# A four-layer state-space network: softplus in another PSUM buffer, side work in turns, and a last epilogue in four streams

## The chip, the cores and the metric

The kernel runs on one core of a Trainium2 chip: TensorE (PE), VectorE (DVE), ScalarE (ACT), GpSimd (POOL), and SyncE (SP), which issues the DMAs. The metric is the time of one execution in device microseconds (us); lower is better. The kernel is written with tiles and pools. A scheduler at build time puts the instructions of each engine in an order, chooses the buffer of each tile and adds the waits; the engines then work through their fixed queues.

## The reference

Eight images of 48 x 48 positions and 96 channels pass through four layers, each `x = x + ss2d(group_norm(x))`. Cut to what matters, a layer computes:

```python
xz = x @ in_proj_w.T                       # 96 -> 2 * 192
xc, z = split(xz)
xc = silu(depthwise_conv3x3(xc) + conv_b)
xs = four sequences of xc: row order, column order, both reversed
dts, B, C = split(xs @ x_proj)             # rank 6 or 16, then 16, 16
delta = softplus(dts @ dt_proj + bias)
h = exp(delta * A) * h + delta * u * B     # along 2304 positions, 16 states
y = sum over states of h * C, + D * u
y = layer_norm(sum of the four directions) * silu(z)
x = x + y @ out_proj_w.T
```

The last layer writes the same scan as `decay * cumsum(dB_u / (decay + 1e-12))` with `decay = exp(cumsum(delta * A))`. With these inputs, decay is so small after the first positions that the kernel computes the sums at the ends of each sequence alone; a flag checks this on the chip, and only where it fails the whole last layer is run again.

## The kernel before

Images go in pairs: 4 layers with 4 pairs each, named `(l, p)`. The 192 inner channels of two images are three tiles of 128 partitions: 128 channels of each image, and the last 64 channels of both.

A pair has three parts. The **prologue** (line 276) loads x, computes the group norm, the input projection, the 3 x 3 convolution (nine matmuls for each of five row chunks and each of three tiles, line 301), silu, and the x projections, whose results go to DRAM. The **units** are the scans, for each tile, phase and direction (12 groups). In layers 0 to 2 a unit is one state of a chunk of 768 positions. In the last layer (`Edge`, line 825) a group has four units, each with four states of 192 positions (`EDGE`): `decay` makes four exponentials da (880), `spread` makes rq with Ln and Exp (887, 888) and spreads B over the partitions with four matmuls into a PSUM tile b (893), `scan` multiplies twice on DVE (898, 899), runs four scans (901) and multiplies twice on POOL (905, 906), and `add_up` sums into acc with identity matmuls (913), four units later (`LAG`). `prepare` (563) computes softplus for a group: a matmul (585), six ACT operations (590 to 601), two on POOL (603, 604), one on DVE (607), a copy to dl (609) and the product du (611, 614); in the last layer a scan over dl follows (839). The **epilogue** (942) takes the pair's y from DRAM in 16 chunks of 144 positions: a first sum over channels subtracts the mean (956 to 962), copy and square (996, 997), a second sum over channels, Ln and Exp (1006, 1007), product (1009), scale (1012), gate projection (1018, 1022), silu (259, with a table load ahead of it and one behind, 260), product (1031), output projection with transposition (1057 to 1059), copy (1063), and two DMAs to the output.

`run` (1114) writes all this in one program order. In unit k it readies unit k+1, scans unit k and adds up unit k-4. Then it takes side steps: each `yield` in a prologue or epilogue ends one step. `behind` is the epilogue of the pair before, `ahead` the prologue of the next. `side_step` takes a step of that side which holds a PSUM bank (its last step yielded True), or of the one that has made the smaller share of its total; a prologue step can also be refused (`GATED`) until the units have come to tile t. In layers 0 to 2 there is at most one side step for each unit, in the last layer ten. What remains is drained at the last group of a pair. After all units, the last pair's epilogue is drained by itself (line 1211).

PSUM[...]: pool `pacc` one buffer of two banks (acc), `pb` two buffers of two banks (b), `psum` two buffers of one bank (`bank()`), which serve softplus, prologue and epilogue. In SBUF the epilogue has two buffers each for ex and ey (`sm2`) and one each for exn and eyc (`sm1`); `tmp` has three large buffers, which the prologues use.

`keep_order(a, b)` (1100) adds an order between all neighbours on each engine, over the instructions number a to b as written. `mark()` notes the current number. It is called before the first unit, and at unit 0 of every pair in the last layer; `keep_order(*marks[:2])` so holds layers 0 to 2 to the written order. What lies outside, the scheduler may reorder.

Of the kernel before, what the change touches and what calls it, by code (L numbers as in the profile page):

```python
# [102 lines left out]
def ss2d_layers_kernel(ctx: ExitStack, tc: tile.TileContext, x_in, consts, weights, out):  # L103
# [158 lines left out]
    def bank():  # L262
        return psum.tile([P, BANK], F32, name="ps", tag="ps")
# [299 lines left out]
    def prepare(c):  # L563
        l, p, t, ph, d = c.l, c.p, c.t, c.ph, c.d
        ly, s = layers[l], state[l, p]
        k, r = ph + 2 * d, ly.rank
        c.dl = ddpool.tile([P, SCAN], F32, name="dl", tag="dl")[:, : c.m]
        c.du = ddpool.tile([P, SCAN], F32, name="du", tag="du")[:, : c.m]
        u = s["u"][t]
        if ph == 1:  # L570
            u = u.rearrange("p (h w) -> p w h", w=W)
        if c.dts is None:
            load_dt(c)
        dts = c.dts
        for z in range(0, c.m, HALF):
            m = min(HALF, c.m - z)
            at = slice(z, z + m)

            ps = bank()
            v = ps[:, :m]  # L580
            for b in c.batches:
                q0 = 32 * b if t == 2 else 0
                o = ps[64 * b : 64 * b + 64] if t == 2 else ps
                chans = slice(P, DIN) if t == 2 else slice(0, P)
                nc.tensor.matmul(  # L585
                    o[:, :m], ly.dtw[q0 : q0 + r, k, chans], dts[q0 : q0 + r, at],
                    start=True, stop=True,
                )
            yield
            nc.scalar.activation(v, v, AF.Identity, bias=ly.column(t, C_DTB + k))  # L590


            e = sm1.tile([P, HALF], F32, name="e", tag="e")[:, :m]
            nc.scalar.activation(e, v, AF.Abs)
            nc.scalar.activation(e, e, AF.Exp, scale=-1.0)
            yield
            lg = sm1.tile([P, HALF], F32, name="lg", tag="lg")[:, :m]
            nc.scalar.activation(lg, e, AF.Ln, bias=ones)
            w1 = sm1.tile([P, HALF], F32, name="w1", tag="w1")[:, :m]
            nc.scalar.activation(w1, e, AF.Identity, bias=ones)  # L600
            nc.scalar.activation(w1, w1, AF.Identity, bias=minus)  # L601
            yield
            nc.gpsimd.tensor_sub(lg, lg, w1)  # L603
            nc.gpsimd.tensor_add(lg, lg, e)  # L604
            yield
            yield
            nc.vector.scalar_tensor_tensor(v, v, 0.0, lg, ALU.max, ALU.add)
            yield
            nc.scalar.copy(c.dl[:, at], v)
            if ph == 0:  # L610
                nc.vector.tensor_mul(c.du[:, at], v, u[:, c.c0 + z : c.c0 + z + m])  # L611
            else:
                r0 = (c.c0 + z) // H
                nc.vector.tensor_mul(
                    c.du[:, at].rearrange("p (w h) -> p w h", h=H),
                    v.rearrange("p (w h) -> p w h", h=H),
                    u[:, r0 : r0 + m // H, :],
                )
            if z + m == c.m and l == NLAYER - 1:
                c.sum_up()  # L620
            if z + m == c.m:
                yield
# [29 lines left out]
    class Chunk:  # L652
# [47 lines left out]
        def load(self, n):  # L700

            s, m, at = state[self.l, self.p], self.m, slice(self.c0, self.c0 + self.m)
            if n == 0:
                self.brow = rpool.tile([2 * NR, SCAN], BF16, name="brow", tag="brow")
                for j, b in enumerate(self.batches):
                    nc.sync.dma_start(
                        self.brow[NR * j : NR * j + NR, :m],
                        s["xb"][self.ph, b, :, self.d, :, at],
                    )
            row = 2 * layers[self.l].rank + 2 * NS * self.d + NS + n  # L710
            self.cb[n] = cb = cbpool.tile([P, SCAN], F32, name="cb", tag="cb")
            for b in self.batches:
                o = cb[64 * b : 64 * b + 64] if self.t == 2 else cb
                rows = s["xd"][self.ph, b, row : row + 1, at]
                nc.sync.dma_start(
                    o[:, :m], rows.to_broadcast([64 if self.t == 2 else P, m])
                )
# [221 lines left out]
                nc.sync.dma_start(s["yd"][t], y)  # L939


    def epilogue(l, p):
        ly, s = layers[l], state[l, p]
        gn, yd, src = s["gn"], s["yd"], x_store(l, p)
        dst = x_store(l + 1, p) if l + 1 < NLAYER else None
# [5 lines left out]
        def over_channels(ps, z, own, own_2, tiles):  # L951


            for t in tiles:
# [4 lines left out]
                for b in range(2):  # L959
                    o = ps[half(b), 2, :]  # L960
                    nc.tensor.matmul(o, off[:, 0:64], z[:, b, :], start=True, stop=False)  # L961
                    nc.tensor.matmul(o, own_2[:, half(b)], z[:, 2, :], start=False, stop=True)

        def three():
            return bank()[:, : 3 * EM].rearrange("p (t m) -> p t m", t=3)

        loaded = {}

        def load(i):
            at = slice(ECHUNKS[i][0], sum(ECHUNKS[i]))  # L970
            x = sm2.tile([DM, 2, EM], F32, name="ex", tag="ex")
            nc.sync.dma_start(x, src[:, :, at].rearrange("b c m -> c b m"))
            y = sm2.tile([P, 3, EM], F32, name="ey", tag="ey")
            nc.sync.dma_start(y, yd[:, :, at].rearrange("t p m -> p t m"))
            loaded[i] = x, y

        load(0)
        for _ in range(3):
            yield
        for i, (c0, m) in enumerate(ECHUNKS):  # L980
            at = slice(c0, c0 + m)
            x, y = loaded.pop(i)

            ps = three()
            over_channels(ps, y, centre, centre_22, (0, 1))
            yield True
            over_channels(ps, y, centre, centre_22, (2,))
            xn = sm1.tile([DM, 2, EM], F32, name="exn", tag="exn")
            for b in range(2):
                nc.scalar.activation(  # L990
                    xn[:, b, :], x[:, b, :], AF.Identity,
                    bias=gn[:, b, 1:2], scale=gn[:, b, 0:1],
                )
            yield True
            yc = sm1.tile([P, 3, EM], F32, name="eyc", tag="eyc")
            nc.scalar.copy(yc, ps)
            nc.scalar.activation(y, ps, AF.Square)
            yield
# [22 lines left out]
            for b in range(2):  # L1021
# [1 line left out]
                    ps[half(b), 2, :], ly.inw[:, DIN + P : 2 * DIN], xn[:, b, :],  # L1023
                    start=True, stop=True,
                )
            if i + 1 < len(ECHUNKS):
                load(i + 1)
            yield True
            silu(ps, ps)
            yield True  # L1030
# [18 lines left out]
                continue  # L1049

            q = m // 2
            ps = bank()[:q, : 4 * DM].rearrange("q (h b c) -> q h b c", h=2, b=2)
            for h in range(2):
                z = slice(h * q, h * q + q)
                for b in range(2):
# [10 lines left out]
                    out[2 * p + b, at, :].rearrange("(h q) c -> q h c", h=2), st[:, :, b, :]  # L1066
                )
            yield
        del state[l, p]


    def drain(g):
        for _ in g:
            pass
# [22 lines left out]
    def mark():  # L1097
        marks.append(len(tc._region_blocks()[0].instructions))

    def keep_order(a, b):  # L1100

        last = {}
        info = mybir.DependencyInfo(mybir.DependencyClass.NoSync, mybir.DependencyReason.DATA)
        for i in tc._region_blocks()[0].instructions[a:b]:
            if i.engine in ENGINES:
                if i.engine in last:
                    tc.add_manual_dep(i, last[i.engine], info, reason="order")
                last[i.engine] = i.name
# [5 lines left out]
    def run(pairs, short):  # L1114
# [53 lines left out]
        for k, ((l, p, unit), c, n) in enumerate(todo):  # L1168
            at = pairs.index((l, p))
            following = pairs[at + 1] if at + 1 < len(pairs) else None  # L1170
            if l in short and unit == 0:
                mark()
            per = NS // QUAD if l in short else NS
            all_units = len(groups) * (per if l in short else len(SCANS) * per)
            place["tiles"] = 3 * unit // all_units
            if done:
                behind, done = Side(epilogue(*done), 195), None
            if unit == LAG and following:
                ahead = Side(begin(*following), 300)
            if n == 0:  # L1180
                drain(coming)
                if unit + per == all_units:
                    drain(behind.g)
                    drain(ahead.g)
                coming_to = chunks.index(c) + 1
                coming = prepare(chunks[coming_to]) if coming_to < len(chunks) else iter(())
            if n == max(0, per - 1 - DECAYS):
                drain(coming)
            if n == 10 and coming_to + 1 < len(chunks):
                z = chunks[coming_to + 1]  # L1190
                if (z.l, z.p) == (l, p):
                    load_dt(z)
            busy = collected()
            get_ready(k + 1)
            catch_up()
            c.scan(n)
            if k >= LAG:
                (bl, bp, _), b, bn = todo[k - LAG]
                b.add_up(bn)
                if todo[k - LAG + 1][0][:2] != (bl, bp):  # L1200
                    done = bl, bp
            step(coming)

            for _ in range(10 if l in short else 0 if busy else 1):
                side_step(rest) or side_step(behind, ahead)
        for _, c, n in todo[-LAG:]:
            collected()
            c.add_up(n)
            catch_up()
        collected()  # L1210
        drain(epilogue(*pairs[-1]))

    last = NLAYER - 1
    run([(l, p) for l in range(NLAYER) for p in range(NPAIR)], (last,))

    keep_order(*marks[:2])


    every = sm1.tile([P, 1], F32, name="every", tag="every")
# [102 lines left out]
```

## Time and profile before

| what | us |
|---|---|
| time, median of 3 runs | 21290.81 (21287.53 to 21323.55) |
| time of the profiled execution | 21306.41 |
| its span | 21304.6 |
| mean granted clock of TensorE in it | 0.944 |

The profile comes from one execution, taken by the hardware profiler. Its page gives the busy time of each engine over the span, and the span in 40 equal slices, about 533 us each, in which a digit is the busy share in tenths. The trace behind it can be asked for stretches (start and end, length, then for each engine busy time and number of instructions in it, then the granted clock of TensorE as a share of full speed, the mean busy share of the DMA engines, and GB/s), for the waits (which engine at which line waited for which, in total, how often, and the longest), for the chain of waits that ended last (start, duration, engine and line), and for single instructions. An fp32 matmul has two records in the trace. The dearest groups of the last layer's lines, from 18400 us to the end (busy us, mean ns; the rest of the row is idle time before them):

| line | what | records | busy us | mean ns |
|---|---|---|---|---|
| 301 | PE, convolution, 128 x 480 | 990 | 412.4 | 557 |
| 901 | DVE, scan, 128 x 192 | 768 | 363.7 | 532 |
| 913 | PE, acc | 1536 | 355.5 | 378 |
| 905, 906 | POOL, products, 128 x 768, each | 192 | 347.4 | 1816, 1810 |
| 880 | ACT, da, 128 x 192 | 768 | 293.0 | 442 |
| 887, 888 | ACT, rq, 128 x 768 | 192, 192 | 176.1, 158.7 | 925, 833 |
| 898, 899 | DVE, products with b | 192, 192 | 181.4, 182.3 | 955, 955 |
| 259, 260 | ACT, table loads | 101, 101 | 129.6, 129.6 | 1283, 1283 |

Records overlap each other, so a mean times a count can exceed the busy time.

### The profile page before, as it was taken

The numbers are of one execution on the slowest core, as the hardware profiler recorded it, in microseconds if no ns is written. First come the engines' busy times: TensorE is split into PE (matmuls) and PEld (weight loads), VectorE is DVE, ScalarE is ACT, GpSimd is POOL, SyncE is SP. The second block draws the span as 40 slices with busy tenths as digits, with TensorE's granted clock in tenths as the row PEclk, the third lists the DMA queues.
The fourth block names the chain that finished last, engine by engine and source line by source line (L and its number), as shares of the span: only waits on it lengthen the run. The fifth ranks groups of instructions, "written<-read, shape, count | busy, mean of one in ns | idle before, by whom it ended". The sixth has DMA issues, their size and how long they took to land. (4 is left out here: it accounts for less than half of the span.)

```text
span 21304.6 us, 229326 instructions
## 1 busy us (share of the span) xinstructions
PE 18651.1 (88%) x64610; PEld 9183.5 (43%) x64610; DVE 18839.5 (88%) x15938; ACT 13518.2 (63%) x23969; POOL 17988.3 (84%) x11081
## 2 busy tenths in 40 slices
PE   8988988998998998998998988988988988988886
PEld 3333443443443443443443443443443443444555
DVE  6999999999999999999999999999999999997453
ACT  5655666666666665665665666665665665666776
POOL 5989898888899899899898889889889888896442
PEclk8999999999999999999999999999999999999887
DMA  4666676676676676676676666666666666664221
GB/s 136 195 190 192 190 196 192 188 192 193 190 198 195 187 200 193 187 202 196 187 200 192 191 193 195 186 194 194 186 195 192 187 194 191 189 193 124 78 72 52
DMA packets 1707633, 3832.97 MB, mean 180 GB/s; under 512 B 238448, under 2 KB 575216, under 8 KB 1693168
## 3 DMA queue, kind: packets, MB, share of 16 engines
q1 hardware_dynamic: 1706352, 3818.21, 61.5%
q8 instruction: 521, 8.54, 0.2%
q14 instruction: 760, 6.23, 0.1%
HBM read 3665.08 MB, written 152.27 MB: 179 GB/s over the span
## 5 line engine op out<-in xcount | busy, mean ns | idle before, releaser
L804 PE MATMUL acc<-cb,cst 128*128 128x384 f32 x27648 | 10772.4, 519 | 0.0
L768 POOL TENSOR_TENSOR cb<-cb,da 128x768 f32<-128x768 f32 x5184 | 9350.0, 1813 | 1586.3 <-DVE da L759 953.8
L804 PEld LDWEIGHTS acc<-cb,cst 128*128 128x128 f32 x27648 | 5031.9, 197 | 3972.4 <-issue 1530.2
L759 DVE TENSOR_TENSOR_SCAN da<-da,carry,b 128x768 f32<-128x768 f32 x3456 | 6267.3, 1813 | 219.0 <-DVE b L755 1.4
L755 DVE TENSOR_TENSOR b<-du,b 128x768 f32<-128x768 f32 x5184 | 4910.0, 947 | 789.6 <-PE b L743 780.1
L726 ACT ACTIVATE da<-dl,a 128x768 f32<-128x768 f32 x5184 | 4770.6, 926 | 94.0 <-POOL cb L768 61.2
L743 PE MATMUL b<-brow,pick 48*128 48x512 bf16 (+3 forms) x10368 | 2660.3, 338 | 1516.2 <-DVE da L759 1184.7
L726 ACT ACTIVATE b<-dl,a 128x768 f32<-128x768 f32 x1728 | 1560.5, 903 | 2927.1 <-DVE da L759 2673.6
L768 POOL TENSOR_TENSOR cb<-cb,bb 128x768 f32<-128x768 f32 x1728 | 3133.2, 1813 | 188.1 <-issue 63.6
L698 POOL TENSOR_TENSOR bb<-bb,du 128x768 f32<-128x768 f32 x1728 | 3131.4, 1812 | 124.5 <-DMA bb<-xd 78.8
L759 DVE TENSOR_TENSOR_SCAN da<-da,b 128x768 f32<-128x768 f32 x1728 | 3029.5, 1753 | 107.4 <-DVE b L755 0.9
L743 PEld LDWEIGHTS <-pick 48*128 48x128 bf16 (+1 forms) x10368 | 667.2, 97 | 4345.3 <-DVE da L759 2285.7
L759 DVE TENSOR_TENSOR_SCAN bb<-b,carry,bb 128x768 f32<-128x768 f32 x1152 | 2069.7, 1797 | 9.1 <-ACT b L726 6.1
L301 PE MATMUL ps<-pad,diag 128*128 128x480 f32 (+1 forms) x4320 | 1995.8, 560 | 17.0 <-DVE du L611 11.5
L650 ACT COPY carry<-da 128x1 f32<-128x1 f32 x3456 | 626.9, 181 | 1068.6 <-DVE da L759 1055.7
L590 ACT ACTIVATE ps<-ps,w 128x384 f32<-128x384 f32 (+1 forms) x912 | 496.6, 545 | 1115.0 <-PE ps L585 1114.4
L301 PEld LDWEIGHTS ps<-pad,diag 128*128 128x128 f32 x4320 | 807.4, 192 | 721.1 <-issue 293.4
L603 POOL TENSOR_TENSOR lg<-lg,w 128x384 f32<-128x384 f32 (+1 forms) x912 | 891.5, 977 | 196.7 <-ACT w L601 196.6
L759 DVE TENSOR_TENSOR_SCAN bb<-b,bb 128x768 f32<-128x768 f32 x576 | 999.2, 1735 | 15.5 <-ACT b L726 11.9
L585 PE MATMUL ps<-dts,w 6*128 6x384 f32 (+5 forms) x2432 | 819.7, 522 | 182.0 <-DVE du L611 65.9
L604 POOL TENSOR_TENSOR lg<-lg,e 128x384 f32<-128x384 f32 (+1 forms) x912 | 889.3, 975 | 71.2
L798 PE MATMUL acc<-y,cst 128*128 128x384 f32 x1008 | 625.3, 751 | 275.2 <-ACT y L819 176.2
(141 smaller groups left out, 17322.1 us busy)
## 6 DMA issues: line engine op xcount, KB each, us to landing
cb<-xd SPq DMA_DIRECT2D x4736, 384.0 KB
cb<-xd SPq DMA_DIRECT2D x4736, 192.0 KB
bb<-xd SPq DMA_DIRECT2D x1152, 384.0 KB
bb<-xd SPq DMA_DIRECT2D x1152, 192.0 KB
yd<-y SPq DMA_DIRECT2D x48, 1152.0 KB
ey<-yd SPq DMA_DIRECT2D x256, 216.0 KB
brow<-xb SPq DMA_DIRECT2D x576, 72.0 KB
ex<-xs SPq DMA_DIRECT2D x256, 108.0 KB
```

The costliest lines, as they stand in the source:

```text
L301: nc.tensor.matmul(ps[:, :m], ly.diag[:, int(t == 2), j, :], pad[:, r0 + dy : r0 + dy + nr, dx : dx + W], start=(j == 0), stop=(j == 8),)
L585: nc.tensor.matmul(o[:, :m], ly.dtw[q0 : q0 + r, k, chans], dts[q0 : q0 + r, at], start=True, stop=True,)
L603: nc.gpsimd.tensor_sub(lg, lg, w1)
L604: nc.gpsimd.tensor_add(lg, lg, e)
L650: nc.scalar.copy(*late_act.pop(0))
L698: nc.gpsimd.tensor_mul(b, b, self.du)
L726: nc.scalar.activation(da, self.dl, AF.Exp, scale=columns_of(self.l, self.t, self.ph, self.d, n))
L743: nc.tensor.matmul(b[:, z : z + zm], w, self.brow[:k, z : z + zm], start=True, stop=True)
L755: nc.vector.tensor_mul(b, self.du, b)
L759: nc.vector.tensor_tensor_scan(way(h), way(da), way(b), start, ALU.mult, ALU.add)
L768: nc.gpsimd.tensor_mul(c, c, h)
L804: nc.tensor.matmul(self.acc[:, a, : self.m // 2], ident, c[:, a, :], start=False, stop=(n == NS - 1 and not self.turns),)
```

## The change

All of it concerns the last layer. In `prepare`, softplus of a group of 192 positions takes its PSUM tile from `pb` (tag b) in place of `psum`. In each unit of the last layer, `ahead` gets eight tries and `behind` five, one after the other in turns, in place of ten steps by share. `epilogue` gets `part` and `parts`: a stream takes every fourth chunk. Streams 0 and 1 take their PSUM banks from `psum`, 2 and 3 from `pb`; stream 0 keeps its small buffers and its load ahead, while streams 1 to 3 have x, xn, y and yc in one buffer of `tmp` and load at the start of a chunk. The last epilogue runs as four such streams, one step of each in turn. `mark()` is called ahead of them and after them, and a second `keep_order` takes the marks with index 2 and 3. Epilogues of other pairs have `part=0, parts=1`.

```diff
@@ -576,7 +576,8 @@
-            ps = bank()
+
+            ps = pb.tile([P, 2 * BANK], F32, name="b", tag="b") if c.m == EDGE else bank()
             v = ps[:, :m]
@@ -939,7 +940,8 @@
-    def epilogue(l, p):
+    def epilogue(l, p, part=0, parts=1):
+
...
+        def own_bank():
+            return bank() if part < 2 else pb.tile([P, 2 * BANK], F32, name="b", tag="b")
+
         def three():
-            return bank()[:, : 3 * EM].rearrange("p (t m) -> p t m", t=3)
+            return own_bank()[:, : 3 * EM].rearrange("p (t m) -> p t m", t=3)
 
         loaded = {}
 
         def load(i):
             at = slice(ECHUNKS[i][0], sum(ECHUNKS[i]))
-            x = sm2.tile([DM, 2, EM], F32, name="ex", tag="ex")
+            if part:
+                w = tmp.tile([P, 10 * EM], F32, name="ew", tag="tmp")
+                x, xn = (
+                    w[:DM, a * EM : a * EM + 2 * EM].rearrange("p (b m) -> p b m", b=2)
+                    for a in (0, 2)
+                )
+                y, yc = (
+                    w[:, a * EM : a * EM + 3 * EM].rearrange("p (t m) -> p t m", t=3)
+                    for a in (4, 7)
+                )
+            else:
+                x = sm2.tile([DM, 2, EM], F32, name="ex", tag="ex")
+                y = sm2.tile([P, 3, EM], F32, name="ey", tag="ey")
+                xn = yc = None
             nc.sync.dma_start(x, src[:, :, at].rearrange("b c m -> c b m"))
-            y = sm2.tile([P, 3, EM], F32, name="ey", tag="ey")
             nc.sync.dma_start(y, yd[:, :, at].rearrange("t p m -> p t m"))
-            loaded[i] = x, y
-
-        load(0)
+            loaded[i] = x, y, xn, yc
+
+        mine_of = range(part, len(ECHUNKS), parts)
+        load(part)
         for _ in range(3):
             yield
-        for i, (c0, m) in enumerate(ECHUNKS):
+        for i in mine_of:
+            c0, m = ECHUNKS[i]
             at = slice(c0, c0 + m)
-            x, y = loaded.pop(i)
+            if i not in loaded:
+                load(i)
+            x, y, xn, yc = loaded.pop(i)
...
-            if i + 1 < len(ECHUNKS):
-                load(i + 1)
+            if not part and i + parts < len(ECHUNKS):
+                load(i + parts)
...
-            ps = bank()[:q, : 4 * DM].rearrange("q (h b c) -> q h b c", h=2, b=2)
+            ps = own_bank()[:q, : 4 * DM].rearrange("q (h b c) -> q h b c", h=2, b=2)
...
-            for _ in range(10 if l in short else 0 if busy else 1):
+            if l in short:
+                for i in range(8):
+                    side_step(ahead)
+                    if i < 5:
+                        side_step(behind)
+            elif not busy:
                 side_step(rest) or side_step(behind, ahead)
...
         collected()
-        drain(epilogue(*pairs[-1]))
+        mark()
+        streams = [epilogue(*pairs[-1], part, 4) for part in range(4)]
+        while streams:
+            streams = [g for g in streams if next(g, g) is not g]
+        mark()
 
     last = NLAYER - 1
     run([(l, p) for l in range(NLAYER) for p in range(NPAIR)], (last,))
 
     keep_order(*marks[:2])
+    keep_order(*marks[2:4])
```

Left out are the lines that make exn and eyc only where the stream has none, and the release of a pair's state once all its streams have ended.

More of the change, by code (lines that the diff above doesn't have):

```diff
@@ L987, in epilogue @@
             over_channels(ps, y, centre, centre_22, (2,))
-            xn = sm1.tile([DM, 2, EM], F32, name="exn", tag="exn")
+            if xn is None:
+                xn = sm1.tile([DM, 2, EM], F32, name="exn", tag="exn")
             for b in range(2):
@@ L994, in epilogue @@
             yield True
-            yc = sm1.tile([P, 3, EM], F32, name="eyc", tag="eyc")
+            if yc is None:
+                yc = sm1.tile([P, 3, EM], F32, name="eyc", tag="eyc")
             nc.scalar.copy(yc, ps)
@@ L1068, in epilogue @@
             yield
-        del state[l, p]
+        state[l, p]["left"] = state[l, p].get("left", parts) - 1
+        if not state[l, p]["left"]:
+            del state[l, p]
     def drain(g):
```

## The prediction

> **What bounds the kernel now.** I read the page's busy shares and 40 slices first, to find where the touched code runs.
>
> ```profile
> PE 18651.1 (88%) x64610; PEld 9183.5 (43%) x64610; DVE 18839.5 (88%) x15938; ACT 13518.2 (63%) x23969; POOL 17988.3 (84%) x11081
> ...
> PE   8988988998998998998998988988988988988886
> DVE  6999999999999999999999999999999999997453
> ACT  5655666666666665665665666665665665666776
> ```
>
> For 36 slices VectorE is at nine tenths and ScalarE near six. The last three or four slices are another regime: DVE falls to 7, 4, 5 and 3, ACT rises to 7. That is the last layer, the only place that the edit touches, about 1,915 of 21,305 us. So I cut it by pair (the 192 scans of line 901 in each give the borders) and took the busy times of each stretch: pairs 0, 1, 2, 3, then the last epilogue.
>
> ```profile
> 19390.00:19790.00 400.00, 348.08 (x1762) 235.79 (x1763) 219.23 (x384) 319.10 (x588) 185.53 (x125) 0.91 0.31 86
> 19790.00:20240.00 450.00, 372.36 (x2016) 257.68 (x2016) 225.55 (x394) 351.95 (x652) 191.43 (x134) 0.89 0.27 75
> 20240.00:20690.00 450.00, 375.44 (x1992) 259.12 (x1991) 227.59 (x398) 350.24 (x660) 192.50 (x135) 0.87 0.26 73
> 20690.00:21063.00 373.00, 252.08 (x1603) 207.87 (x1603) 213.06 (x375) 291.29 (x556) 183.95 (x119) 0.80 0.24 67
> 21063.00:21305.00 242.00, 158.88 (x1042) 135.40 (x1041) 20.36 (x35) 118.24 (x190) 1.80 (x1) 0.73 0.13 34
> ```
>
> Columns: length, PE, weight loads, DVE, ACT, POOL, clock, DMA. In pairs 0 to 2 PE (83%) and ACT (78%) are both near full and wait for each other; in pair 3 ACT leads; in the tail nobody does, and the clock is 0.73. The chain of waits of the tail shows why:
>
> ```profile
> 21140.12 1.28 ACT L259
> 21141.85 1.02 ACT eyc L1012 x2
> 21153.83 1.28 ACT L259
> 21155.55 1.02 ACT eyc L1012 x2
> 21167.51 1.28 ACT L259
> ```
>
> The table load for silu comes every 13.7 us, once a chunk: a chain PE, ACT, PE, ACT, DVE, ACT, PE with one chunk in flight. The waits, first of the tail, then of the pairs (us in total, times, longest):
>
> ```profile
> DVE eyc L1009 <- ACT ps L1007: 172.1, 16, 16.2
> ```
> ```profile
> PE b L893 <- DVE rq L901: 80.3, 37, 7.8
> ...
> PE ps L585 <- DVE du L611: 18.5, 4, 4.8
> ```
> ```profile
> ACT dl L609 <- DVE ps L607: 53.0, 27, 5.8
> ```
>
> The second says that PE, in order, already waits for a free buffer of b; the third is PE waiting for a bank that softplus holds; the last is ScalarE standing in softplus for GpSimd and VectorE.
>
> **What the skill says.** The Trainium skill, "TensorE: Matmul & The Clock Gate", What's actually happening: the array runs at half rate until about 3.4 us of sustained work. The trace agrees: the 24 output records of a tail chunk (L1057 to L1059), after an idle PE, come every 0.16 us, inside busy stretches (at 19930.4 us) every 0.083 us. "ScalarE: Activation LUTs", What ACT_TABLE_LOAD costs: 1,283 ns and a drain of about 1,380. The trace has 1,283 ns and no drain beside it: the silu starts 0.01 us after its load. "Perfetto Trace Analysis", Tensor Engine Instruction (MATMUL, LD_WEIGHTS): ScalarE, VectorE and GpSimd are strict FIFO. So the place of an instruction in its queue decides what a wait blocks, which the waits above bear out.
>
> **Tail.** One chunk costs, from the timeline at 21150 to 21164 us: first over_channels A 2.0 us of PE, second B 1.9, gate C 1.16, output 3.8 cold or 1.9 warm. ScalarE: two exn 0.91, copy and square 1.06, Ln and Exp 1.11, scale 1.01, load, silu, load 3.08, eo 0.47; sum 7.64. Sixteen chunks at 13.67 are 219 us. The four streams advance in turns, and the changed program's instruction order on PE and ScalarE is phase by phase: four A's, four B's, four C's, four silus, four outputs. From the end of the fourth silu: DVE and the last output 2.7 us; four A's 7.9; four B's 7.6; last Ln, Exp 2.2; four scales 4.05; four silus 12.3 less the closing load 1.28, 11.0. That is 35.5 us for four chunks. copy, square, C and exn lie beside PE's or ScalarE's longer phase. Streams 1 to 3 have no prefetch: their loads (324 KB, where 216 KB took 2.65 us on the chain) begin when their buffer is free, and are covered by the next A of stream 0. I add 2.5 us a round for what of this and of the cold clock shows: 38 us, four rounds 152, and 5 at the start for four loads in place of one. Gain 219-157 = 62. Bounds: 35.5 gives 77; 43 (outputs cold at 1.9 more, loads exposed by 4, and 1.6 for refilled queues) gives about 46. All 32 table loads remain.
>
> **Which instructions keep their order.** run() marks the first unit once, then the first unit of every pair of the last layer, then both ends of the streams: numbers 0, 1 to 4, 5 and 6. keep_order(*marks[2:4]) hence spans pair 1 of the last layer, from its first unit to pair 2's, and not the streams; these the scheduler orders, in phases as told. In pair 1 every queue, SP's too, now follows the written order.
>
> **Pairs 0 and 2.** Before, ten side steps a unit were shared by progress: 40 units x 10 = 400, while a prologue has 259 and an epilogue 195 (counted yields). The remaining 54, among them most of the 44 steps of the x projections, were poured out at unit 44. Slices of 50 us show it (line 901's scans, then all engines):
>
> ```profile
> 20200.00:20250.00 50.00, 3.77 (x8) 0.77 0.31 91
> ```
> ```profile
> 20200.00:20250.00 50.00, 30.94 (x198) 24.15 (x199) 12.78 (x25) 33.05 (x58) 6.47 (x10) 0.77 0.31 91
> ```
>
> There are 8 scans where 192 in 450 us make 21, and PE has 31 of 50 us. After, 8 x 40 and 5 x 40 finish both by unit 44. Filling that hole is worth 20 to 25 us a pair (PE 31 instead of 44 of 50 us, and its follow-up). Against it stands softplus in b: it holds one of two buffers from L585 to L611, 6.8 us in the trace (19912.4 to 19919.2), once in four units, so the next b waits. DVE, 3.8 us a unit in units of 8.7, hides most; I take 1 us a group, 11 groups, +10. Net -12 each. Bounds: -45 (all hidden, the freed bank lets convolution and epilogue overlap), +25 (4 us a group, half the hole).
>
> **Pair 1.** The same hole, -20. In written order softplus stands in one piece: after the silu (3.08) and a convolution's eviction (0.65) come six ScalarE operations 2.4, two GpSimd 1.2, DVE 0.37, ACT 0.30, DVE 0.36: 8.4 us. PE has four convolution matmuls (3.3) before a wait for the bank and three after it, then the b that needs softplus's buffer. It stands about 4 to 6 us; behind it are acc, convolution and the epilogue's matmuls, and ScalarE waits for those. 11 groups x 4.5 = 50. Net +30. Below: nothing more than the hole, if queues run ahead (-30); above: 6 us a group, and 25 us each for the chains of the group norm and of the projections, whose DMAs landed in up to 4.7 us on the chain of waits (+95).
>
> **Pair 3.** No prologue: before, ten steps a unit finished the epilogue by unit 27 at 9.7 us a unit (14.6 us a chunk, the tail's chain again), and 24 units ran at 5.4. After, five steps a unit last to unit 43. ACT's 291 us less 9 bare units at 3.5 is 260 over 39 units, 6.65; at 88% busy 7.56. 39 x 7.56 + 9 x 5.4 = 344 against 373: -30. Bounds -60 (full ScalarE) and 0 (the chain still paces).
>
> Sum: -12+30-12-30-62 = -86. Against the profiled execution, 21306.4 (span 21304.6 and 1.8 around it), 21220; that run was 15.6 over the median of 21290.8, so I forecast 21205.
>
> **Rivals.** (1) The two free banks let PE run warm and full in all pairs: PE's 372 us at 96% is 388 instead of 450, of which I would believe half: pairs 0 to 2 -35, -10, -35, pair 3 -45, tail -70: -195, 21096. For it: clock 0.88 while PE is 83% busy. Against: ScalarE's 351 us are nearly as long. (2) The order is kept in the wrong place and costs +95 in pair 1, the rest as forecast: -21, 21270. For it: four engines at two thirds coupled without any reordering. Against: the same mechanism holds for the first three layers, at nine tenths. (3) Slower: softplus in b's buffer. Its place is the b after L585, its price a PE that stands until L611; at 4.5 us in each of 44 groups, that is +198, less the holes' 60 and the tail's 62, with pair 3's gain gone: +76, 21367. It decides from about 2.8 us a group. For it: 80.3 us of waiting for b already; against: DVE's slack of nearly 5 us a unit.
>
> **Numbers.** Forecast 0.54, (1) 0.17, (2) 0.17, (3) 0.12. The forecast's own range is -150 to -25. 0.2% is 43 us, which a measurement can just tell. Faster: 0.47 of the forecast, all of (1), a quarter of (2): 0.68. Slower: (3) mostly, 0.11. Same: 0.21. The range, 21100 to 21300, leaves half of (1)'s lower side and (3) out.
>
> **What would show it.** Right: loads of silu in fours with 35 to 43 us between groups and a clock above 0.8 in the tail; pair 1 longer than pair 2; silu evenly through pair 3; no slice with 8 scans before a pair's end. Wrong: a tail above 200 us (loads late), pair 1 shorter than before, or in pairs 0 and 2 PE waits for DVE rq or du before b far above 80 us in all.

## The result, and the profile after

The changed kernel takes 21279.55 us (median of 12 runs, 21253.59 to 21305.26) against 21290.11 us for the kernel before (12 runs): a ratio of 0.9995, with a 95% interval of 0.9987 to 1.0002. No change can be told. The forecast was 21205, in a range that holds the result; the rival nearest to it is the second, 21270.

The time is the same, but its parts are not. I take the borders from the DVE scans in the trace: a pair lasts from its first scan to the next pair's first, pair 3 to the start of its last scan, the tail from there to the end of the span. Every row comes from one profiled execution. Three of the runs below (e1, e2, e8) have all their pairs written alike, and they repeat them within 0.5 us.

| us | start of the layer | pair 0 | pair 1 | pair 2 | pair 3 | tail | span |
|---|---|---|---|---|---|---|---|
| before | 19396.3 | 420.9 | 437.0 | 440.5 | 368.2 | 241.7 | 21304.6 |
| changed | 19381.3 | 418.1 | 551.5 | 421.1 | 355.0 | 160.3 | 21287.4 |
| difference | -15.0 | -2.8 | +114.5 | -19.4 | -13.2 | -81.4 | -17.2 |

The start varies from 19377 to 19407 us among the runs below, whose first three layers are alike, so its -15 is noise. The last layer by itself, from its start to the end of the span, changed by -2 us. The page's slices of the changed kernel answer to those of before:

```profile
PE   8988998998998998998998988988998988988787
...
DVE  6999999999999999999999999999999999996454
ACT  5555666666666665665666666665665666666677
```

They say little: the last digits of PE rose from 8, 6 to 8, 7, and those of DVE moved from 7, 4, 5, 3 to 6, 4, 5, 4. An average over 530 us hides a pair that lost 115 us beside a tail that won 81. The stretches by pair and tail show it (length, then PE, weight loads, DVE, ACT and POOL, clock, DMA):

```profile
19381.00:19799.00 418.00, 362.31 (x1780) 237.79 (x1779) 224.00 (x386) 340.20 (x643) 192.18 (x132) 0.89 0.27 77
19799.00:20351.00 552.00, 412.17 (x1997) 280.59 (x1998) 235.24 (x401) 351.65 (x647) 193.63 (x140) 0.82 0.22 61
20351.00:20772.00 421.00, 374.29 (x2001) 253.75 (x1999) 223.64 (x388) 341.21 (x646) 192.41 (x132) 0.91 0.27 79
20772.00:21127.00 355.00, 255.54 (x1606) 208.74 (x1606) 213.83 (x373) 291.10 (x551) 178.16 (x115) 0.83 0.27 76
21127.00:21287.00 160.00, 121.61 (x1042) 109.16 (x1042) 19.88 (x36) 110.16 (x184) 2.60 (x2) 0.86 0.19 50
```

In pair 1 the engines do the work of pair 2 (1,997 matmul records against 2,001), but no engine is above 75% busy, the clock is 0.82, and PE needs 412 us where pair 2's needs 374. In the tail PE's 1,042 records take 122 us where they took 159 before, at a clock of 0.86 in place of 0.73. The ratio of the clocks would account for 24 of these 37 us, if busy time went with it. Pair 1's waits in the changed kernel, first PE's and then ScalarE's (us in total, times, longest):

```profile
PE b L894 <- DVE du L615: 28.5, 6, 9.4
PE b L894 <- DVE du L612: 25.3, 6, 5.0
```
```profile
ACT eo L1086 <- PE ps L1082: 37.5, 12, 6.2
ACT ps L1029 <- PE ps L964: 27.7, 10, 4.5
ACT eyc L1019 <- PE ps L964: 25.2, 7, 7.0
```

The first two are the wait that the prediction named, b behind softplus's buffer: 53.8 us in 12 groups. But ScalarE stands longer for PE, 90.4 us in three places of the epilogue's chain. Both engines wait, in good part for each other. The experiments had to say which of this is cause.

### The profile page after: what moved, and what is told of

Read it like the earlier page. It is cut to its first block, busy times and chain, and to the rows that moved or that the text cites. A ratio compares the mean times of both kernels' runs of the same rounds, so it can differ in the third digit from the quotient of the medians.

```text
span 21287.4 us, 229081 instructions
## 1 busy us (share of the span) xinstructions
PE 18667.0 (88%) x64610; PEld 9175.5 (43%) x64610; DVE 18857.0 (89%) x15938; ACT 13514.9 (63%) x23971; POOL 17989.0 (85%) x11081
## 5 line engine op out<-in xcount | busy, mean ns | idle before, releaser
L591 ACT ACTIVATE ps<-ps,w 128x384 f32<-128x384 f32 x864 | 478.0, 553 | 1083.8 <-PE ps L586 1083.2
L586 PE MATMUL ps<-dts,w 6*128 6x384 f32 (+3 forms) x2304 | 786.2, 527 | 155.9 <-DVE du L615 50.8
```

The costliest lines, as they stand in the source:

```text
L586: nc.tensor.matmul(o[:, :m], ly.dtw[q0 : q0 + r, k, chans], dts[q0 : q0 + r, at], start=True, stop=True,)
```

## The experiments

**The second kept order taken away** (e1_free_pair1), from the changed kernel:

```diff
-    keep_order(*marks[2:4])
```

> The changed kernel without its second keep_order; all else as it is. Theory A (the kept order in pair 1 of the last layer is what ate the gain): pair 1 falls from 551 us to 410 to 440, the last epilogue and the other pairs stay as they are (418, 421, 355, tail 160), the whole is 100 to 140 us faster than the changed kernel, near 21165. Theory B (softplus in the buffer of b, with thirteen steps a unit, makes pair 1 long, as it would any pair whose queues run full): pair 1 stays above 510, the whole within 40 us of the changed kernel.

Measured: 21136.84 us, ratio to before 0.9924 (0.9908 to 0.9941). Pairs 420.3, 411.5, 407.0, 352.1, tail 160.4. Theory A holds: the one line costs pair 1 140 us. Of the rest of the table only pair 2 moves clearly, from 421.1 to 407.0, so the order costs the pair behind it another 14. The order adds no instructions that could cost this time: the profile counts 229,081 with it and 229,165 without. The stretch of pair 1 without it:

```profile
19815.00:20226.00 411.00, 367.09 (x1990) 248.83 (x1990) 227.67 (x393) 340.14 (x644) 193.71 (x136) 0.92 0.29 80
```

PE's busy time for nearly the same records falls from 412 to 367 us and the clock rises from 0.82 to 0.92. So 45 of the 140 us are growth of PE's busy time, and not waiting. Busy time multiplied by the clock is 338 us in both, so here the slower clock by itself would give this growth. PE's list of waits in this stretch begins with

```profile
PE acc L914 <- POOL cb L907: 14.9, 12, 2.1
PE b L894 <- DVE rq L902: 8.9, 6, 2.8
```

The two waits for du are gone from it, with softplus still in the buffer of b.

**The order kept where the streams are** (e2_order_on_streams), from the changed kernel:

```diff
-    keep_order(*marks[2:4])
+    keep_order(*marks[5:7])
```

> The changed kernel with the second keep_order moved to the marks with index 5 and 6, the two ends of the four streams. Theory A: pair 1 as in e1_free_pair1 (410 to 440); the last epilogue, phase by phase in the written order as well, stays within 6 us of 160, since the scheduler had already put it in nearly that order. A rival, that the order kept over the streams is worth something of its own: the tail changes by 10 us or more either way.

Measured: 21158.8 us, 0.9937 (0.992 to 0.9953). Pair 1 is 411.5, as without any second order, and only the tail moves: the marks with index 5 and 6 bound the streams. The tail is 183.0 in place of 160.4: the expectation that the order would hardly matter there was wrong, it costs 22.6 us. The tail's waits name the place, first of SP (the DMA queue), then of the engines:

```profile
SPq L1088 <- ACT eo L1086: 134.8, 7, 33.6
```
```profile
ACT ew L1012 <- DMA ew<-xs: 34.5, 12, 20.2
...
PE ps L958 <- DMA ew<-yd: 18.1, 3, 6.1
```

I read this so: in written order the output stores stand ahead of the next round's loads in SP's queue and wait for ScalarE's copies, and the streams without prefetch then wait for their data. No run freed SP alone here. Without the kept order, that wait of SP is 31.4 us in the changed kernel's tail.

**The kernel before with that order alone** (e3_before_ordered):

```diff
     keep_order(*marks[:2])
+    keep_order(*marks[2:4])
```

> The kernel before, with nothing but the second keep_order added (marks 2 to 4, pair 1 of the last layer). Theory A in its wide form (any written order of this layer, kept, stalls the queues): pair 1 grows from 437 us by 60 to 150. Theory A in its narrow form (the kept order hurts by softplus in the buffer of b, on which PE then stands some 54 us, and by steps in turns): pair 1 grows by less than 50. Theory B: unchanged within 15.

Measured: 21437.14 us, 1.0065 (1.0049 to 1.0082). Pair 1 grows from 437.0 to 590.5, the others stay within 9. This is theory A in its wide form: the price is 153 us with softplus in psum and steps by share, so neither of these two edits is needed for it. Pair 1 in the kernel before and in this run:

```profile
19817.00:20254.00 437.00, 365.30 (x1982) 252.75 (x1982) 224.36 (x393) 343.44 (x642) 191.48 (x134) 0.89 0.26 75
```
```profile
19803.00:20394.00 591.00, 428.08 (x1993) 293.31 (x1993) 235.32 (x401) 352.43 (x651) 194.65 (x140) 0.79 0.21 57
```

**The four streams alone** (e5_before_streams): the kernel before with the changed epilogue (`part`, `parts`), but steps by share, softplus in psum and no second order. The line that starts the streams:

```diff
-        drain(epilogue(*pairs[-1]))
+        streams = [epilogue(*pairs[-1], part, 4) for part in range(4)]
+        while streams:
+            streams = [g for g in streams if next(g, g) is not g]
```

> The kernel before with the four streams of the last epilogue alone: steps by share, softplus in psum, no second kept order. The tail should fall from 242 us to 155 to 165 as in the changed kernel, the pairs stay at 421, 437, 440, 368 within 10 each, the whole about 80 us faster than before, near 21210. If the tail's gain needs the other edits, it stays above 180.

Measured: 21222.06 us, 0.9964 (0.995 to 0.9978). The tail is 159.9, the pairs 421.2, 437.0, 439.1, 369.9. The streams bring their 82 us in the tail by themselves, and they leave the pairs as they were.

**Softplus back in psum** (e4_softplus_psum), from e1_free_pair1:

```diff
-            ps = pb.tile([P, 2 * BANK], F32, name="b", tag="b") if c.m == EDGE else bank()
+            ps = bank()
```

> e1_free_pair1 with softplus back in psum, so that prologue, epilogue and softplus share two banks again; eight and five steps in turns and the streams stay. Theory C (softplus in the buffer of b frees the bank that the turns need): pairs 0 to 2 rise from 420, 411, 407 by 15 to 40 each, pair 3 from 352 to 360 to 370. Theory D (the turns alone bring it, the place of softplus is indifferent or even costs PE some waits before b, as the prediction had it at +10 a pair): all pairs within 8 us of e1_free_pair1, or up to 12 shorter.

Measured: 21148.7 us, 0.9935 (0.992 to 0.9951). Pairs 407.6, 417.0, 423.0, 342.4: their sum is 1590.0 against 1590.9. Neither theory fits pair by pair: pair 2 rises by 16, pairs 0 and 3 fall by 13 and 10.

**Softplus in the buffer of b alone** (e7_before_softplus_b): the kernel before with the same edit the other way round, from `bank()` to `pb`.

> The kernel before with softplus in the buffer of b and nothing else. Theory C: little changes, since one side at a time holds a bank; pairs 421, 437, 440, 368 within 10. Theory D with its price: each pair 5 to 25 us longer, as the next b waits for softplus. A gain of more than 10 us a pair would say that softplus's bank, not the sharing of steps, was the limit before.

Measured: 21235.76 us, 0.9973 (0.9963 to 0.9982). Pairs 406.4, 404.0, 408.3, 387.2: a gain of 14 to 33 in pairs 0 to 2 and a loss of 19 in pair 3. So in pairs 0 to 2 softplus's bank held the kernel before back, as the last sentence of the expectation allowed. In pair 3, where nothing is gained, softplus itself waits for a buffer of b:

```profile
PE b L585 <- DVE rq L901: 21.6, 8, 5.8
```

With the sum of the four pairs, the two edits now stand as a square:

| sum of the pairs, us | softplus in psum | softplus in the buffer of b |
|---|---|---|
| ten steps by share | 1666.6 (before) | 1605.9 |
| eight and five in turns | 1590.0 | 1590.9 |

Each edit alone gains 61 to 77 us, both together 76. They are two ways to the same gain and do not add. (The kernels of the lower row also have the streams, which leave the pairs alone.)

The traces show where the gain sits. Before, the last unit of pair 2, from its first scan to pair 3's, lasts 45.6 us: it is the hole that the prediction saw. It lasts 16.2 us with softplus in the buffer of b (e7), 11.0 with the turns (e4) and 8.3 with both (e1). Pair 3's first scan needs the softplus of pair 3's first group, and this is its matmul in the kernel before and in e7:

```profile
20681.43 1.64 PE L585 MATMUL ps<-dts,w 6*128 6x192 f32 x4
```
```profile
20553.14 0.59 PE L585 MATMUL b<-dts,w 6*128 6x192 f32 x2
```

Pair 3's first scan starts at 20694.7 and 20596.6 us. In the kernel before this softplus comes 13 us ahead of the scan, late in the hole; in the buffer of b it comes 43 us ahead. With turns few side steps are left to be poured out there.

**One table switch a round** (e8_one_table_switch), from e1_free_pair1; the last stream's silu alone switches back:

```diff
-            silu(ps, ps)
+            if part < parts - 1:
+                nc.scalar.activation(ps, ps, AF.Silu)
+            else:
+                silu(ps, ps)
```

> e1_free_pair1, and in the last epilogue's streams the tables are switched back only after the fourth stream's silu: 8 table loads in the tail where there were 32. If the tail's rounds are paced by ScalarE from the scales to the fourth silu, as the chain shows (33.7 us a round), six loads of 1.28 us fall out of each: 7.7 us a round, 31 us in all, tail near 130, the whole near 21107. If PE or the loads of x and y are next right behind, less than 15 us.

Measured: 21143.79 us, 0.993 (0.9916 to 0.9943). The tail is 153.3 in place of 160.4: 24 table loads, 30.8 us of ScalarE, brought 7.1 in the tail, and nothing that the time of the whole shows (21136.84 without this edit). The chain of waits of the changed kernel has the silus in a row, four switches to a round:

```profile
21192.92 2.72 ACT ew L1035 x6
21195.66 1.28 ACT L259
21197.49 1.28 ACT L260
...
21226.57 2.72 ACT ew L1035 x6
```

In the edited kernel loads of y come into the chain instead:

```profile
21022.75 1.28 ACT L1053
21032.43 3.69 DMA ew<-yd
...
21055.09 1.28 ACT L1053
```

So something else was right behind, as the expectation's second half said: the rounds are 32.2 to 33.6 us here, 33.7 without the edit. The chain goes through a load of y in two of the three rounds.

**Which queue of pair 1.** Three kernels (e9_order_without_sp, e10_order_act_only, e11_order_pe_only) keep its order on some engines only, one execution each:

```diff
-    def keep_order(a, b):
+    def keep_order(a, b, engines=ENGINES):
...
-            if i.engine in ENGINES:
+            if i.engine in engines:
...
-    keep_order(*marks[2:4])
+    keep_order(*marks[2:4], ENGINES[:4])
```

These lines are e9; e10 and e11 have `ENGINES[2:3]` (ScalarE) and `ENGINES[:1]` (PE) in the last line.

> The changed kernel, but the order in pair 1 is kept on PE, DVE, ACT and POOL only; the DMA queue stays with the scheduler. If the in-order DMA queue is what stalls pair 1 (its output stores wait 206 us for ScalarE's copies ahead of the loads of dts and cb), pair 1 falls from 551 to below 480. If the compute engines' kept order stalls it, pair 1 stays above 520.

> The changed kernel with the order in pair 1 kept on ScalarE alone. ScalarE is the engine with the longest waits for PE in the ordered pair (eo, Ln, copy: some 90 us of the 115). If its kept order is the cause, pair 1 stays above 490 us of 551; if PE's is, it falls below 450, against 411 with no kept order.

> The changed kernel with the order in pair 1 kept on PE alone. If PE's kept order is the cause (54 us of waits for softplus's buffer ahead of b, and convolution, epilogue and acc behind them), pair 1 stays above 490 us; if ScalarE's is, below 450. Both between 440 and 500 would say that each queue brings a part and they add up.

| order kept in pair 1 on | pair 1, us |
|---|---|
| none (e1) | 411.5 |
| PE (e11) | 477.2 |
| ACT (e10) | 490.2 |
| PE, DVE, ACT, POOL (e9) | 528.8 |
| these and SP (changed kernel) | 551.5 |

SP's part is 23 us. ScalarE's order alone costs 79 and PE's alone 66. Neither falls below 450, and 490.2 lies on the border of the second expectation: it is the case that the third one named, each queue brings a part. But the parts don't simply add up, as 66 and 79 are more than the 117 of the four engines together, and DVE's and POOL's order was not kept alone. With PE alone ordered, no wait for du stands among PE's longest; the longest is for the epilogue's product:

```profile
PE ps L1081 <- DVE eyc L1054: 16.5, 4, 5.4
PE ps L958 <- ACT ey L1020: 9.1, 7, 3.5
```

**A mix of the best stages** (e12_mix), from e1_free_pair1: softplus in psum for pair 3 only, ten steps by share with a prologue, five without, four streams with one switch.

```diff
-            ps = pb.tile([P, 2 * BANK], F32, name="b", tag="b") if c.m == EDGE else bank()
+            ps = pb.tile([P, 2 * BANK], F32, name="b", tag="b") if c.m == EDGE and p < NPAIR - 1 else bank()
...
+            if l in short and not following:
+                for _ in range(5):
+                    side_step(behind)
+            else:
+                for _ in range(10 if l in short else 0 if busy else 1):
+                    side_step(rest) or side_step(behind, ahead)
```

Left out are the lines for the turns, which these replace, and the table switch, which is as in e8.

> A mix of what the runs before showed best, with no second kept order: softplus in the buffer of b and ten steps by share in pairs 0 to 2 (as in e7_before_softplus_b: 406, 404, 408), softplus in psum and five epilogue steps a unit in pair 3 (as in e4_softplus_psum: 342), four streams with one table switch a round (as in e8_one_table_switch: 153). If stages add up, the layer takes 1713 us in place of 1752 in e1_free_pair1, the whole about 40 us less than that, near 21100. If not (pair 3 inherits what pair 2 leaves over), within 10 us of e1_free_pair1.

Measured: 21138.56 us, 0.9929 (0.9916 to 0.9943), as e1_free_pair1 within their spread. Pairs 399.5, 406.6, 436.8, 343.4, tail 159.7. Pair 2 gives back what pairs 0 and 3 won, and the tail keeps 0.7 of e8's 7 us. Stages chosen from different kernels don't add up. In pair 2 the trace shows why: its last unit is back at 43.9 us. Its side steps are written as in e7, but pair 3's first softplus, which is made within pair 2, is in psum again, and it comes 13 us ahead of the scan that needs it (20633.6), as in the kernel before:

```profile
20620.90 1.22 PE L586 MATMUL ps<-dts,w 6*128 6x192 f32 x4
```

Up to the end of pair 2 the two kernels are written alike but for that softplus, so this run tests, without having been meant to, that the hole hangs on its bank. The simplest version that beats both kernels remains the changed kernel without its second kept order.

## Why the prediction came out as it did

The forecast was -86 us, and -10.6 was measured by the medians. That the result lies in the range is owed to the range's width. The forecast's five terms, which sum to -86, measured -2.3 in the profiles. Pair 1 alone is off by 84.5; the errors of the other four cancel by luck.

- **Which instructions keep their order:** right. The second order spans pair 1 and not the streams; e1, e2 and e3 show it.
- **Pair 1, the step that failed.** The kept order was priced as one wait, 50 us behind softplus's buffer, less a 20 us hole closed: +30, with +95 as the bound. Measured +114.5. The wait was sized well (53.8 us), but the loss doesn't need it: e3 pays 153 us without softplus in that buffer, and e11 pays 66 without this wait among PE's longest. What the runs show in its place is the order itself, on more than one queue: 140 us against the same kernel without it, 66 with PE's order alone, 79 with ScalarE's, 23 by SP's beside the others. Left out of the sum was also the clock: nearly the same matmuls took PE 45 us more. Why the written order is that bad stays open. My reading is that each queue takes ten (e3) or thirteen (changed kernel) short steps of two dependent chains between the unit's own work, so that the engines wait for each other in turn; no run varied the number of steps under a kept order.
- **The second rival** had +95 in pair 1 and 21270 in all, which is nearest to the result. The argument against it was that the first layers keep their order at nine tenths busy. But there at most one side step falls to a unit of 2.8 us (19396 us over 12 pairs of 576 units), here up to thirteen to one of 8.6 (411.5 over 48). The two stretches differ, and the first doesn't vouch for the second; no run frees the first layers' order.
- **Tail:** right in kind, -62 against -81.4. The term too large was the round: 38 us assumed, 33.7 measured, which makes 17 of the 19 us. The measured round is below even the 35.5 us that stood before 2.5 were added for late loads and a cold clock.
- **Pairs 0 and 2:** -12 each, measured -2.8 and -19.4, where pair 2 bears 14 us of pair 1's order (-33.5 in e1). The hole did close, but pair 0 paid for it elsewhere: cut into quarters of twelve units by its scans, its last quarter fell from 135.9 to 95.0 us, and its first, which now takes thirteen steps a unit, rose from 67.4 to 101.9. The +10 for softplus in b had the wrong sign in the kernel before: alone it is a gain in pairs 0 to 2 (e7). Beside the turns it is worth nothing either way (1590.9 against 1590.0).
- **Pair 3:** -30, measured -13.2, inside its bounds. The forecast of 344 us was set against 373, read from a window of rounded ends. By its scans pair 3 took 368.2 before, so that 5 us of the miss are this reading, and 355.0 after.
- **The third rival**, softplus in b's buffer makes every pair longer, is refuted for pairs 0 to 2. Pair 3 of e7 does lose 19 us, but not as the rival had it: the list of PE's waits there has no b that waits for du; it has softplus waiting for a buffer of b (21.6 us).

## What to carry to other kernels

A list of marks is only as good as its count of who marks: an order that looks meant for the streams landed on a pair and cost it 140 us (on the streams it cost 22.6, in e2). Test a kept order by itself, above all where many steps of other chains stand between two dependent instructions of one queue. When a drain pours out what is left at the end of a stage, look at what the next stage needs first and whether it must queue behind that. Compare stage by stage when a large edit moves nothing: here a stage that lost 115 us stood beside one that won 81.

## What the runs showed of the hardware

More waiting went with a slower clock: with pair 1's order kept, PE's busy time for about 1,990 records rose from 367 to 412 us, as the granted clock fell from 0.92 to 0.82, which is what the ratio of the clocks gives. In e3 it rose from 365 us at 0.89 to 428 at 0.79, where the ratio of the clocks gives 46 of the 63 us. And taking 30.8 us of table loads out of a ScalarE that led the chain of waits shortened the tail by 7.1 us in e8, and in e12, with the same edit, by 0.7.
